# Searching the maxima of odd steps one step ahead, writing small maps in halves, moving keys and first values: one change to a two-layer convolution and attention kernel

## The chip, the cores and the metric

The kernel runs on one core of one Trainium2 chip. Its time is the device time of one execution in microseconds; the median of three runs is shown. The core has five engines with a queue of instructions each: TensorE (PE in the profile, with PEld for weight loads), VectorE (DVE), ScalarE (ACT), GpSimd (POOL) and SyncE (SP), which here only issues transfers. They meet through semaphores: an instruction waits until what it reads is there and what it overwrites has been read.

## The reference, cut to what matters

The input x has 8 images of 256 channels and 64 x 64 pixels, in float32. Two layers follow each other; each normalises its input by groups of 8 channels and adds its result to it.

Layer 0 makes, for every pixel, its own 3 x 3 filter and applies it:

```python
x1, x2, x3 = _conv1x1(x, w1, b1), _conv1x1(x, w2, b2), _conv1x1(x, w3, b3)   # 32, 32, 256 maps
h = jnp.concatenate([x1, unfold3(reflect(x2))], axis=1)
h = relu(bn2(_conv1x1(relu(bn1(h)), cw1)))
w = _conv1x1(h, cw2, cb2).reshape(B, 32, 9, H, W)
out = jnp.einsum('bgskhw,bgkhw->bgshw', x3u, w)      # 9 taps, one filter for 8 channels
```

Layer 1 adds two branches. The first is attention of four heads in a window of 7 x 7 around each pixel, with a position term added to the keys; the second applies two 3 x 3 depthwise convolutions with a relu between them and weighs the result by a softmax over nine branches:

```python
att = softmax(jnp.einsum('bdn,bdkn->bnk', q, uk + upe[None]))
out_att = jnp.einsum('bnk,bdkn->bdn', att, uv)
wts = softmax(jnp.einsum('oc,bchw->bohw', Wfc, x).reshape(b, C, 9, h, w), axis=2)
out_conv = sum over 9 of dwconv(relu(dwconv(x, w1)), w2) * wts
x + rate1 * out_att + rate2 * out_conv
```

## The kernel before, in words

An image is cut into 8 bands of 8 rows; 64 bands in all. Layer 1 works on band g while layer 0 prepares the band 12 ahead of it (`AHEAD`). The first 12 rounds therefore have layer 0 alone, the last 12 have layer 1 alone.

A round of one band has 8 steps: two halves of the channels (ct) times four (m). A step takes two tiles of 8 x 8 queries of two heads. The order of the work is written out by hand, in the loop at the end: every engine gets its instructions in the order in which the program records them, and `after(n, f)` puts f off by n places, of which each step has six (the calls of `advance`). `beside(g, s)` lists what a step carries besides its own work: `head` runs before the exponentials, `mid` in the middle, `end` at the end.

In a step PE makes: at even m the scores of this step and the next, both in one PSUM tile "sco" (L747); two products with the branch weights, "pf" (L883); the transposes of the step before, "ptp" (L784); at even m the weighted values of the two steps before, in a PSUM tile "small" (L796). DVE searches the maximum of each row of masked scores ("prob", "nmax", L761: two searches in a step, one for each head), ACT turns scores into exponentials (L769) and divides them by their sum (L778, after DVE's reciprocal "tot", L776), and turns pf into exponentials "ex" (L888). DVE also does the taps of the two depthwise convolutions ("acc", L840 and L866), and adds the attention to the band's result ("xr", L815).

Beside it stand:

- Layer 0's small maps (`small_maps` and `write_maps`): at step 0 PE makes 32 + 32 maps in the free half of "small" (L332), and ACT writes them to "x2" in eight pieces, four for each half of the band's rows (L347 and L351). POOL then copies border rows and columns (L355 to L364). `hidden_maps` reads x2 one round later (L422).
- Layer 0's 256 maps "p" (L373), half at the end of step 0 and half at step 1; ACT writes them to "x3n" (L378), from where they go to DRAM.
- The taps: at the end of steps 1 to 5 PE makes the filters of two taps, "pw" (L468); DVE multiplies the first at the next place and the second one place later ("prod", L481), POOL adds the products to "xg" (L489).
- Layer 1's keys (`keys`, PE "pk" L703, DVE "kb" L711 and L718), queries ("pq", "qb"), the position term "pe" (`position`, L655 to L661, made for the first image and stored for the others) and values (`values`, PE "pv" L598, ACT "vc" L605), which SP stores to DRAM ("vd", L618 and L622) and loads again as tiles "vt" (L640).

Four PSUM buffers with the tag "gen" go round among pf, ptp, p, pw, pk, pq and pv; "sco" and "small" have one buffer each. In SBUF, "vc" has one buffer and "ex" three.

The changed lines lie in `small_maps` and `write_maps`, `values`, `position`, `beside`, and the loop itself. What sets their order is, for the loop:

```python
prob, nmax = masked(nm, m, sco)         # each step searches its own maxima
for a, po in weighted:
    add_values(*a, po)
ahead = [f() for f in head]
tot = exponentials(nm, prob, nmax)
```

Of the kernel before, what the change touches and what calls it, by code (L numbers as in the profile page):

```python
# [18 lines left out]
P = 128  # L19
# [4 lines left out]
R = 8  # L24
# [63 lines left out]
def conv_layers_kernel(ctx: ExitStack, tc: tile.TileContext, ins: dict, out: bass.AP):  # L88
# [235 lines left out]
    def small_maps(b, i, home):  # L324


        im = images[b]

        p12 = home[:, 2 * P :].rearrange("p (r c) -> p r c", r=R // 2)
        for kt in range(NCT):  # L330
            for u in range(2):
                nc.tensor.matmul(  # L332
                    p12[64 * u : 64 * u + 64], im.w12s[:, kt, :],
                    im.xc[i][:, kt, u * BAND // 2 : (u + 1) * BAND // 2],
                    start=(kt == 0), stop=(kt == NCT - 1),
                )
        return lambda: write_maps(b, i, p12)

    def write_maps(b, i, p12):
        im = images[b]  # L340
        t = im.x2[i] = w0.tile([P, HR, W], F32, tag="x2", name=f"x2_{b}_{i}", bufs=2)
        bias = im.bias
        for u in range(2):
            r, o = u * R // 2, 64 * u
            for q, (dst, src) in enumerate(((1, 0), (0, 0), (0, 1))):
                n = W - (q != 1)
                nc.scalar.activation(  # L347
                    t[32 * q : 32 * q + 32, r + 1 : r + 1 + R // 2, dst : dst + n],
                    p12[o : o + 32, :, src : src + n], AF.Identity, bias=bias[o : o + 32, 0:1],
                )  # L350
            nc.scalar.activation(  # L351
                t[96:128, r : r + R // 2, :], p12[o + 32 : o + 64], AF.Identity, bias=bias[o + 32 : o + 64, 0:1]
            )

        nc.gpsimd.tensor_copy(t[0:32, 1 : 1 + R, 0:1], t[0:32, 1 : 1 + R, 2:3])  # L355
        nc.gpsimd.tensor_copy(t[64:96, 1 : 1 + R, W - 1 : W], t[64:96, 1 : 1 + R, W - 3 : W - 2])

        if i == 0:
            nc.gpsimd.tensor_copy(t[0:96, 0, :], t[0:96, 2, :])
        else:  # L360
            nc.gpsimd.tensor_copy(t[0:96, 0, :], im.x2[i - 1][0:96, R, :])
            nc.gpsimd.tensor_copy(im.x2[i - 1][0:96, R + 1, :], t[0:96, 1, :])
        if i == NB - 1:
            nc.gpsimd.tensor_copy(t[0:96, R + 1, :], t[0:96, R - 1, :])  # L364
# [218 lines left out]
    def values(b, j, half):  # L583

        im = images[b]
        if half == 0:
            im.vc[j] = w1.tile([P, R // 2, C], F32, tag="vc", name=f"vc_{b}_{j}", bufs=1)
        vc, yp = im.vc[j], im.yp[min(j, NB - 1)]  # L590
        first, last, _ = value_rows(j)
        pv = ps.tile([P, 2, C], F32, tag="gen", name=f"pv_{b}_{j}_{half}", bufs=4)
        for g in range(2):
            r = first + 4 * half + 2 * g
            if r >= last:
                break
            for kt in range(NCT):
                nc.tensor.matmul(  # L598
                    pv[:, g], yp[:, kt, r : r + 2].rearrange("p r c -> p (r c)"), wv[:, kt],
                    start=(kt == 0), stop=(kt == NCT - 1),  # L600
                )
            n = g + 1

        def take():
            nc.scalar.copy(vc[:, 2 * half : 2 * half + n], pv[:, :n])  # L605

        return take
# [39 lines left out]
    def position(b, i):  # L647

        first, last = new_keys(i)
        n, a = last - first, i * R + first  # L650
        pe = images[b].pe[i] = w1.tile([P, KW - PAD, W], F32, tag="pe", name=f"pe_{b}_{i}", bufs=1)
        if b:
            nc.sync.dma_start(out=pe[:, :n], in_=kept[i])
            return
        nc.gpsimd.tensor_add(  # L655
            pe[:, :n],
            pecol.unsqueeze(1).to_broadcast([P, n, W]),
            perow[:, a : a + n].unsqueeze(2).to_broadcast([P, n, W]),
        )
        kept[i] = dram.tile([P, n, W], F32, tag=f"pe{i}", name=f"pe_{i}", bufs=1)  # L660
        nc.sync.dma_start(out=kept[i], in_=pe[:, :n])  # L661

    kept = {}

# [259 lines left out]
    def beside(g, s):  # L924

        b, i = divmod(g, NB)
        bn, inx = divmod(g + 1, NB)
        head, mid, end = [], [], []

        early = i in (0, NB - 1)  # L930
        if g >= 0:
            if s == 2:
                mid.append(lambda: keys(b, i, 1) if early else queries(b, i, 1))
            if s == 3 and early:
                head.append(lambda: queries(b, i, 1))
            if s == 3 and not early:
                mid.append(lambda: keys(b, i, 1))
        edge = inx in (0, NB - 1)
        if 0 <= g + 1 < B * NB:
            if s == 5 - edge:  # L940
                mid.append(lambda: position(bn, inx))
            if s == 6:
                mid.append(lambda: keys(bn, inx, 0) if edge else queries(bn, inx, 0))
            if s == 7:
                head.append(lambda: queries(bn, inx, 0) if edge else keys(bn, inx, 0))

        made = [(b, i + 2, (4, 5))] if g >= 0 and i < NB - 1 else []
        if i == NB - 1 and 0 <= b + 1 < B:
            made = [(b + 1, 0, (3, 4)), (b + 1, 1, (5, 7))]
        for bb, j, d in made:  # L950
            if s in d and (j < NB or s == d[0]):
                mid.append(lambda bb=bb, j=j, d=d: values(bb, j, d.index(s)))
            if s == d[1]:
                end.append(lambda bb=bb, j=j: store_values(bb, j))
            if s == d[1] + 1 and j in (0, NB):
                end.append(lambda bb=bb, j=j: mirror_rows(bb, j))
            if s == 7 and j != 1:
                for u in range(NT // 2):
                    end.append(lambda bb=bb, j=j, u=u: value_tile(bb, j, u))
        if g >= 0 and i == 0 and s in (0, 2):  # L960
            for u in (s, s + 1):
                mid.append(lambda u=u: value_tile(b, 1, u))

        nxt = [(b, i + 2, 0)] if g >= 0 and i + 2 < NB else []
        if i == NB - 1 and 0 <= b + 1 < B:
            nxt = [(b + 1, 0, 0), (b + 1, 1, 2)]
        for bb, ii, d in nxt:
            if s == d:
                end.append(lambda bb=bb, ii=ii: load_rows(bb, ii))
            if s in (d + 1, d + 2):  # L970
                end.append(lambda bb=bb, ii=ii, d=d: normalise(bb, ii, s - d - 1))

        alone = g < 0
        if 0 <= g + AHEAD < B * NB:
            bq_, iq = divmod(g + AHEAD, NB)
            if alone and s == 0:
                mid.append(lambda: small_maps(bq_, iq, small_tile(f"{bq_}_{iq}"))())
            if s == (2 if alone else 0):
                (mid if alone else end).append(lambda: value_maps(bq_, iq, 0, alone))
            if s == (3 if alone else 1):  # L980
                mid.append(lambda: value_maps(bq_, iq, 1, alone))
        if 0 <= g + AHEAD - 1 < B * NB and s == (2 if alone else 1):
            bh, ih = divmod(g + AHEAD - 1, NB)

            def hidden():
                parts = hidden_maps(bh, ih, alone)
                if not alone:
                    convs.extend(parts)

            end.append(hidden)  # L990
        if 0 <= g + AHEAD - 2 < B * NB and s in TAPS_AT[g < -1]:
            u = TAPS_AT[g < -1].index(s)
            end.append(
                lambda: tap_weights(*divmod(g + AHEAD - 2, NB), u, g < -1, PRODUCTS_AT[g < -1][u])
            )
        return head, mid, end
# [24 lines left out]
    with tc.manual_schedule():  # L1021
# [17 lines left out]
        for n, f in enumerate(layer1_loads()):  # L1039
            after(4 * STEPS * (3 + n), f)  # L1040

        pending, before, conv, convs = [], None, None, []
        for g in range(-AHEAD, B * NB):
            b, i = divmod(g, NB)
            for s in range(STEPS):
                ct, m = divmod(s, NT // 2)
                head, mid, end = beside(g, s)
                steer(g, s)
                if g >= 0:
                    nm = f"{b}_{i}_{ct}_{m}"  # L1050
                    weighted = []
                    if m % 2 == 0:
# [3 lines left out]
                        small = small_tile(nm)  # L1056
                        weighted, pending = weigh_steps(pending, small), []
                        if s == 0 and g + AHEAD < B * NB:
                            mid.append(small_maps(*divmod(g + AHEAD, NB), small))
                        if s in (4, 6) and convs:  # L1060
                            convs.pop()(small)
                        if before is not None:
                            pending.append((before[:-1], transposed(nm, before[-1])))
                    prob, nmax = masked(nm, m, sco)
                    for a, po in weighted:
                        add_values(*a, po)
                ahead = [f() for f in head]
# [41 lines left out]
                advance()  # L1109
                for f in end:  # L1110
                    f()
                advance()
        for last in (before, None):
            for a, po in weigh_steps(pending, small_tile(f"end{last is None}")):
# [88 lines left out]
```

## Time and profile before

| what | value |
|---|---|
| median of three runs | 3902.41 us (3900.53 to 3902.47) |
| profiled execution, its own time | 3901.4 us |
| its span, first to last instruction | 3899.5 us |
| granted TensorE clock, mean | 0.994 |
| PE busy | 3774.0 us, 97% |
| DVE, POOL, ACT busy | 3415.8, 3118.1, 2809.8 us |
| first scores of layer 1 (L747, band 0) | 233.46 us |
| an ordinary band, with layer 0 beside it | 57.6 us |

The profile is one execution. A row of a view gives an engine, a line, an operation, and the tile that is written and those that are read; "idle before" is how long the engine stood still in front of it, and the name after the arrow is what ended the wait. Ends of matmuls are modelled, so that distances between their starts say more than their durations. All times are microseconds unless marked ns.

### The profile page before, as it was taken

To read this page: it belongs to the slowest core of one execution; us is meant where nothing else is said; L and a number is where in the kernel's file an instruction comes from. 1 tells how busy PE (TensorE), PEld (TensorE's weight loads), DVE (VectorE), ACT (ScalarE), POOL (GpSimd) and SP (SyncE) were. 2 spreads that over 40 slices of the span, in tenths; PEclk is the share of its full clock that TensorE was granted. 3 is DMA by queue.
4 is the path that set the end of the run, shared out by engine and by line. 5 is a ranking of instruction groups with operands and counts; after the bars stand their busy time and mean duration, and the time that the engine had idled before them with its cause. 6 is when DMAs were issued, how large, how long until landed. Compare 5 with 4: busy or idle time off the path is not lost.

```text
span 3899.5 us, 71759 instructions
## 1 busy us (share of the span) xinstructions
PE 3774.0 (97%) x24620; PEld 2112.0 (54%) x24620; DVE 3415.8 (88%) x7125; ACT 2809.8 (72%) x6770; POOL 3118.1 (80%) x2100
## 2 busy tenths in 40 slices
PE   6889999999999999999999999999999999999998
PEld 3445555555555555555555555555555555555554
DVE  6879999889988989899998998989988889978777
ACT  4457777777777777777777777777777777677776
POOL 4768888888987988888888888978988888955665
PEclk9999999999999999999999999999999999999999
DMA  8754544544544543544544544454543543332221
GB/s 247 211 162 128 142 113 126 155 124 113 136 127 131 148 120 104 151 137 118 145 112 136 143 124 116 132 145 119 139 113 102 145 123 101 89 94 81 78 66 37
DMA packets 438926, 490.14 MB, mean 126 GB/s; under 512 B 62016, under 2 KB 324256, under 8 KB 438304
## 3 DMA queue, kind: packets, MB, share of 16 engines
q1 hardware_dynamic: 421984, 469.79, 43.4%
q10 hardware_dynamic: 16576, 15.76, 1.3%
q8 instruction: 194, 3.18, 0.3%
q14 instruction: 172, 1.41, 0.1%
HBM read 343.76 MB, written 145.10 MB: 125 GB/s over the span
## 4 chain that ended last, share of the span: by engine, by line
PE 38%; POOL 22%; DVE 20%; ACT 10%; issue 5%; DMA 4%; SPq 0%; ACTq 0%; POOLq 0%; DVEq 0%
PE pf L883 18%; POOL xg L489 10%; POOL ex L1099 7%; DVE prod L481 6%; DVE rec L904 4%; DVE acc L866 4%; PE small L796 3%; ACT x L347 3%; PE pv L598 3%; PE ptp L784 3%; PE sco L747 3%; PE pq L681 2%; PE pk L703 2%; DMA x<-x3n 2%; ACT ex L888 2%
## 5 line engine op out<-in xcount | busy, mean ns | idle before, releaser
L883 PE MATMUL pf<-yp,c_wfc 128*128 128x512 f32 x4096 | 1916.3, 594 | 16.7 <-ACT ex L888 10.3
L489 POOL TENSOR_TENSOR xg<-xg,prod 128x1024 f32<-128x1024 f32 x549 | 1201.0, 2188 | 108.7 <-DVE prod L481 82.7
L883 PEld LDWEIGHTS pf<-yp,c_wfc 128*128 128x128 f32 x4096 | 738.6, 190 | 715.7 <-issue 628.4
L1099 POOL TENSOR_TENSOR ex<-ex,ex 128x1024 f32<-128x1024 f32 x384 | 908.2, 2365 | 68.7 <-ACT ex L888 65.2
L840 DVE SCALAR_TENSOR_TENSOR acc<-yp,c_chan,acc 128x504 f32<-128x504 f32 (+3 forms) x1104 | 775.8, 703 | 63.3 <-ACT acc L831 42.9
L481 DVE SCALAR_TENSOR_TENSOR prod<-pw,c_par,x3q 128x1040 f32<-128x1040 f32 x576 | 737.3, 1287 | 92.3 <-PE pw L468 47.8
L866 DVE SCALAR_TENSOR_TENSOR acc<-hid,c_chan,acc 128x504 f32<-128x504 f32 (+3 forms) x1024 | 751.5, 734 | 18.1
L888 ACT ACTIVATE ex<-pf 128x512 f32<-128x512 f32 x1024 | 602.3, 588 | 220.7 <-PE pf L883 204.4
L769 ACT ACTIVATE prob<-prob,nmax 128x196 f32<-128x196 f32 x1024 | 459.2, 451 | 205.2 <-DVE nmax L761 204.9
L778 ACT ACTIVATE prob<-prob,tot 128x196 f32<-128x196 f32 x1024 | 413.0, 452 | 262.0 <-DVE tot L776 259.9
L905 POOL TENSOR_TENSOR tot<-tot,rec 128x256 f32<-128x256 f32 x254 | 185.7, 731 | 413.4 <-DVE rec L904 407.3
L904 DVE RECIPROCAL rec<-tot 128x256 f32<-128x256 f32 x256 | 445.8, 1741 | 8.2 <-POOL tot L899 6.6
L786 ACT COPY pt<-ptp 112x512 f32<-112x512 f32 x511 | 295.0, 577 | 111.3 <-PE ptp L784 110.8
L761 DVE CUSTOM_DVE_ANT_0 prob<-sco,c_mask 128x196 f32<-128x196 f32 x1024 | 324.8, 355 | 27.1 <-PE sco L747 27.0
L784 PEld LDWEIGHTS ptp<-ident,prob 128*112 128x112 f32 x2044 | 227.3, 133 | 184.8 <-issue 154.7
L784 PE MATMUL ptp<-ident,prob 128*112 128x128 f32 x2044 | 319.5, 279 | 0.2 <-ACT vc L605 0.2
L796 PEld LDWEIGHTS small<-pt,vt 112*64 112x64 f32 x8144 | 258.5, 138 | 83.5 <-issue 75.4
L796 PE MATMUL small<-pt,vt 112*64 112x64 f32 x8144 | 294.1, 225 | 7.2 <-DMA vt<-vd 7.2
L373 PE MATMUL p<-xc,w3s 128*128 128x512 f32 x512 | 248.1, 608 | 12.6 <-ACT ex L888 12.6
L598 PE MATMUL pv<-c_wv,yp 128*128 128x256 f32 x1056 | 252.3, 381 | 1.7 <-ACT yp L570 1.7
L899 POOL TENSOR_SCALAR tot<-tot 128x512 f32<-128x512 f32 x127 | 243.6, 1918 | 11.1
L468 PEld LDWEIGHTS pw<-h2n,c_c 128*128 128x128 f32 x1152 | 176.1, 192 | 138.2 <-issue 122.3
(136 smaller groups left out, 4655.4 us busy)
## 6 DMA issues: line engine op xcount, KB each, us to landing
vt<-vd SPq DMA_DIRECT2D x512, 112.0 KB
x3q<-x SPq DMA_DIRECT2D x128, 264.0 KB
xc<-in_x SPq DMA_DIRECT2D x64, 512.0 KB
xg<-in_xg SPq DMA_DIRECT2D x64, 512.0 KB
yp<-x SPq DMA_DIRECT2D x128, 256.0 KB
xr<-x SPq DMA_DIRECT2D x64, 512.0 KB
out_x<-xr SPq DMA_DIRECT2D x64, 512.0 KB
xs<-in_x SPq DMA_DIRECT2D x57, 512.0 KB
```

The costliest lines, as they stand in the source:

```text
L481: nc.vector.scalar_tensor_tensor(prod[:, :, :RUN], pw[:, j, :RUN].unsqueeze(1).to_broadcast([P, SHARE, RUN]), par[:, PCB2 + k : PCB2 + k + 1],
L489: nc.gpsimd.tensor_add(im.xg[i], im.xg[i], rows(prod))
L769: nc.scalar.activation(prob[:, h, :NKEY], prob[:, h, :NKEY], AF.Exp, bias=nmax[:, h : h + 1], scale=-1.0, accum_out=tot[:, h : h + 1],)
L778: nc.scalar.activation(prob[:, h, :NKEY], prob[:, h, :NKEY], AF.Copy, scale=tot[:, h : h + 1])
L784: nc.tensor.transpose(ptp[:, h, ch], prob[:, h, ch * CHUNK : (ch + 1) * CHUNK], ident)
L796: nc.tensor.matmul(po[half[h], :, t * TQ : (t + 1) * TQ], im.vt[i + ch, m][:n, t, (2 * ct + h) * HD : (2 * ct + h + 1) * HD], pt[:n, h, ch ...
L840: nc.vector.scalar_tensor_tensor(o, yp[:, ct, ra + dr : rb + dr, ca + dc : cb + dc], chan[:, ct, CW1 + k : CW1 + k + 1], o, ALU.mult, ALU.add,
L866: nc.vector.scalar_tensor_tensor(o, hid[:, ra + dr : rb + dr, ca + dc : cb + dc], chan[:, ct, CW2 + k : CW2 + k + 1], o, ALU.mult, ALU.add,)
L883: nc.tensor.matmul(pf, wfc[:, kt, 2 * m + j, ct * P : (ct + 1) * P], images[b].yp[i][:, kt, PAD : PAD + R], start=(kt == 0), stop=(kt == N ...
L888: nc.scalar.activation(ex[:, j].rearrange("p (r c) -> p r c", r=R), pf, AF.Exp)
L904: nc.vector.reciprocal(rec, v)
L1099: after(4, lambda ex=ex, exb=exb: nc.gpsimd.tensor_add(ex, ex, exb))
```

## The change

Five things move; no computation is added or removed. Every engine issues the same instructions as before, and POOL in the same order.

1. Maxima. At the end of each even step, after its `end` work is recorded, the maxima of the odd step that follows are searched; the odd step uses them. On DVE this changes places only at steps 3 and 5, where the two searches now stand in front of the first tap's product (L481).
2. Small maps. `small_maps` returns a function of the half. In rounds with layer 1 the first half of the maps is written at step 0, the second at step 1, ahead of that step's other `mid` work; POOL's copies follow the second half.
3. Keys. In bands that are neither first nor last of an image, the keys of the second half of the channels move at step 3 from `mid` to `head`: pk stands on PE ahead of pf and ptp, and DVE's kb ahead of two taps and the reciprocal.
4. First values. In the round before band 0, the values of band 1 take their second half at step 6 instead of 7, ahead of the queries, and their stores follow at the end of step 6; their tile vc takes a buffer of "ex".
5. Position. The store of pe is put off by nine places, so that on SP it comes after the stores of vd, in band 0 after the loads of x3q.

```diff
+        im.x2[i] = w0.tile([P, HR, W], F32, tag="x2", name=f"x2_{b}_{i}", bufs=2)
-        return lambda: write_maps(b, i, p12)
+        return lambda u: write_maps(b, i, p12, u)
...
-    def write_maps(b, i, p12):
+    def write_maps(b, i, p12, half):
...
-        for u in range(2):
+        for u in half:
...
+        if half[-1] == 0:
+            return
...
-            im.vc[j] = w1.tile([P, R // 2, C], F32, tag="vc", name=f"vc_{b}_{j}", bufs=1)
+            tag, bufs = ("ex", 3) if (b, j) == (0, 1) else ("vc", 1)
+            im.vc[j] = w1.tile([P, R // 2, C], F32, tag=tag, name=f"vc_{b}_{j}", bufs=bufs)
...
-        nc.sync.dma_start(out=kept[i], in_=pe[:, :n])
+        after(9, lambda: nc.sync.dma_start(out=kept[i], in_=pe[:, :n]))
...
             if s == 3 and not early:
-                mid.append(lambda: keys(b, i, 1))
+                head.append(lambda: keys(b, i, 1))
...
-            made = [(b + 1, 0, (3, 4)), (b + 1, 1, (5, 7))]
+            made = [(b + 1, 0, (3, 4)), (b + 1, 1, (5, 7 if g >= 0 else 6))]
...
-                mid.append(lambda: small_maps(bq_, iq, small_tile(f"{bq_}_{iq}"))())
+                mid.append(lambda: small_maps(bq_, iq, small_tile(f"{bq_}_{iq}"))((0, 1)))
...
+                if s == 1:
+                    mid, maps = maps + mid, []
...
-                            mid.append(small_maps(*divmod(g + AHEAD, NB), small))
+                            write = small_maps(*divmod(g + AHEAD, NB), small)
+                            mid.append(lambda write=write: write((0,)))
+                            maps.append(lambda write=write: write((1,)))
...
-                    prob, nmax = masked(nm, m, sco)
+                    prob, nmax = masked(nm, m, sco) if m % 2 == 0 else odd
...
+                if g >= 0 and m % 2 == 0:
+                    odd = masked(f"{b}_{i}_{ct}_{m + 1}", m + 1, sco)
```

More of the change, by code (lines that the diff above doesn't have):

```diff
@@ L336, in small_maps @@
                 )
-        return lambda: write_maps(b, i, p12)
-    def write_maps(b, i, p12):
+        im.x2[i] = w0.tile([P, HR, W], F32, tag="x2", name=f"x2_{b}_{i}", bufs=2)
+        return lambda u: write_maps(b, i, p12, u)
+    def write_maps(b, i, p12, half):
         im = images[b]
-        t = im.x2[i] = w0.tile([P, HR, W], F32, tag="x2", name=f"x2_{b}_{i}", bufs=2)
-        bias = im.bias
-        for u in range(2):
+        t, bias = im.x2[i], im.bias
+        for u in half:
             r, o = u * R // 2, 64 * u
@@ L1040, in conv_layers_kernel @@
             after(4 * STEPS * (3 + n), f)
-        pending, before, conv, convs = [], None, None, []
+        pending, before, conv, convs, maps = [], None, None, [], []
         for g in range(-AHEAD, B * NB):
```

## The prediction

> **What bounds the kernel now.** I read four views in turn. First the page: its opening line and the row of busy time.
>
> ```profile
> span 3899.5 us, 71759 instructions
> PE 3774.0 (97%) x24620; PEld 2112.0 (54%) x24620; DVE 3415.8 (88%) x7125; ACT 2809.8 (72%) x6770; POOL 3118.1 (80%) x2100
> ```
>
> TensorE is the bound: 97% busy, and the slices say 9 tenths from the fourth on. So an edit is worth only what it takes out of the remaining waits of PE. Second, who PE waited for; the columns are microseconds in total, times, longest.
>
> ```profile
> PE p L373 <- ACT ex L888: 12.6, 52, 0.9
> PE small L796 <- DMA vt<-vd: 7.2, 2, 6.7
> PE pf L883 <- DVE prod L481: 6.4, 6, 1.1
> PE sco L747 <- DVE kb L718: 5.2, 29, 0.2
> ```
>
> The first line occurs 52 times: once in each of the first 52 bands, just those that still prepare layer 0. Third, one ordinary band (829.0 to 886.6) in order of time, PE and then ACT (start, duration, engine, line).
>
> ```profile
> 837.46 1.88 PE L883 MATMUL pf<-yp,c_wfc 128*128 128x512 f32 x4
> 839.18 0.60 PE L784 MATMUL ptp<-ident,prob 128*112 128x128 f32 x4
> 839.96 1.98 PE L373 MATMUL p<-xc,w3s 128*128 128x512 f32 x4 [0.18 <-ACT ex L888]
> 841.78 1.88 PE L883 MATMUL pf<-yp,c_wfc 128*128 128x512 f32 x4
> ```
>
> ```profile
> 835.48 1.40 ACT L347 ACTIVATE x<-small,bias 32x252 f32<-32x252 f32 x3
> 836.89 0.46 ACT L351 ACTIVATE x<-small,bias 32x256 f32<-32x256 f32 x1
> 837.36 1.43 ACT L347 ACTIVATE x<-small,bias 32x252 f32<-32x252 f32 x3
> 838.82 0.47 ACT L351 ACTIVATE x<-small,bias 32x256 f32<-32x256 f32 x1
> 839.31 0.60 ACT L888 ACTIVATE ex<-pf 128x512 f32<-128x512 f32 x1
> ```
>
> The page's idle column understates a wait, since ends on PE are modelled; I take distances between starts. ptp to p is 0.78 us here; ptp to a product that waits for nothing is 0.43 (853.78 to 854.21, same band). p to pf is 1.82; four matmuls elsewhere take 1.72 (837.46 to 839.18). So this place costs 0.35 + 0.10 = 0.45 us. Its cause stands in the ACT rows: eight small-map writes run from 835.48 to 839.29 ahead of the exponential that frees the PSUM buffer which p needs. Fourth, the queue of transfers in the first band.
>
> ```profile
> 224.64 0.32 SPq L661 DMA_DIRECT2D pe<-pe  x1
> 225.06 1.32 SPq L618 DMA_DIRECT2D vd<-vc  x2
> 240.86 5.62 SPq L640 DMA_DIRECT2D vt<-vd  x8
> 246.59 1.33 SPq L618 DMA_DIRECT2D vd<-vc  x2
> 247.97 4.07 SPq L622 DMA_DIRECT2D vd<-vc  x6
> 252.75 3.12 SPq L640 DMA_DIRECT2D vt<-vd  x4
> ```
>
> SP issues without a gap from 225 to 256; PE wants the last four tiles at 248.8 and gets the first at 255.78, the second at 256.95.
>
> [...] I therefore price starts, not busy time. [...] the exponential whose input is long ready starts 0.02 us after the eighth write. [...] here a value tile takes 3.0 us from issue to use (252.75 to 255.78).
>
> **Maps in halves.** Moved: four of eight writes per band, 4 x 0.47 = 1.9 us of ACT, from step 0 to step 1 behind the normalised probabilities. Added: nothing. The exponential then starts at 837.4 and ends at 838.0; p is wanted at 839.61. The wait goes. Summed over starts, ptp to p and p to pf exceed 0.43 and 1.72 by 0.45 us in 43 ordinary bands (19), and by 0.7 to 1.1 in eight at image edges or beside them (6): 25 us. Band 0 is counted below. Queued behind the moved writes are x3n, an exponential and the next hid. ACT from 839.31 to 843.05 runs 3.74 us without a gap; starting 1.9 earlier it runs the same 3.74 (nmax was ready at 837.5, tot waits for ACT alone, the product pf ends by 839.3), then the four writes, so x3n starts where it did, near 843.0. Waiting for the second half are two things: "small", single-buffered, which PE writes again at 844.89 - 0.45 = 844.4, a slack of 1.4 us; and POOL's four copies of border rows, now about 843.1 to 844.2 instead of 837.9 to 839.6. POOL idles 5.29 us there until 844.87, so the copies cost nothing; hid, which reads their rows, starts at 846.5. Without these covers the price is the lateness itself, per band.
>
> **Maxima earlier.** Two searches (2 x 0.28 us plus a 0.08 us readout, 0.65 in all) pass one tap product (1.21 us) at steps 3 and 5. The same DVE work; ACT's exponentials of these steps can start 1.2 us sooner, the product and POOL's addition 0.65 later. No PE wait above names nmax. PE's wait for the next scores' buffer gains room. I take 0; bounds -3 us (the product's buffers come free late: the third line of PE's waits) to +5 (a DVE that had idled for pw fills the gap, so the second product of step 5 ends sooner).
>
> **Keys at the head of step 3.** pk passes pf and ptp (1.72 + 0.43 us earlier on PE), and its four DVE operations, 0.65 + 3 x 0.15 = 1.1 us, now stand ahead of two depthwise taps and the reciprocal. In ordinary bands sco waits for kb: pw to sco is 0.79 (857.65 to 858.44) against 0.55 (843.49 to 844.04) where it waits for nothing, 27 times 0.24 = 6.5 us. After the change DVE does two searches, two products and the keys from 852.6: 0.65 + 2.4 + 1.1 is 856.8, before sco at about 858. The 6.5 goes. The price: the reciprocal, ACT's second exponential of step 3 and oc come up to 1.6 us later; PE next needs that buffer 3 us later. Unseen cost: 0 to 3 us; I take 0.
>
> **First values moved.** vc of band 1 gets a slot of "ex", so ACT need not wait 9.0 us (until 231.07) for the stores of vc of band 0; the second half of its product goes ahead of pq. The store of pe goes nine places later, so vd's stores need not wait for POOL's pe (224.64) but only for the copy of vc at 220.7. SP then issues: 8 stores of vd 4.6 us, xr 0.5, six x3q 3.9, pe 0.4, mirrors 1.9, the 8 stores of band 1 (5.5), xs 0.6, four x 3.3, eight tiles 5.6: the last four begin at about 247.0 instead of 252.75, and with the 3.0 to 3.2 us from issue to use PE has both by 250.9 instead of 256.95. PE itself starts band 0 two microseconds sooner (sco at 231.3 for 233.46, after qb, no longer behind vc), which the wait swallows. Gain 6; bounds 2 (only PE's earlier start, if SP stays clogged) to 8. In bands 1 to 7 pe's store, 0.4 us of SP, now follows eight stores of vd; pe is read from DRAM only an image later, so nothing waits.
>
> **Sum.** 25 + 6.5 + 6 = 37.5 us. At image edges DVE (first band) and POOL (last band) set PE's waits; both have their early idle shortened (DVE waits 2.55 us for tot at step 1, POOL 5.29), so the gain should pass through, though not all. I take off 1.5 for that: 36. The profiled execution took 3901.4, 1.9 over its span; the median of the runs is 3902.41, 1.0 above it. 3902.4 - 36 is 3866.
>
> **Rivals.** (A) The freed time comes back as waits for DVE or POOL, whose work per band is unchanged: in an ordinary band they are busy 52.4 and 49.6 of 57.6 us. For: the waits of pf for prod, and DVE runs without a gap through most of a first band. Against: both idle in steps 0 and 1. It would keep a third of the 25, and the rest: 3902 - 20 = 3882. (B) Slower: the second half of the maps is late, and PE waits for "small" at step 2 of every band. The slack is 1.4 us; each microsecond beyond costs 52. It decides from 0.9 us of stall (0.9 x 52 = 47 eats 38 + 8): the writes would have to end 2.3 us later than reckoned. At 1.5 us of stall: 3902 + 78 - 36 = 3944. Against: no gap in ACT's run between. (C) The transfers do not matter and the p wait only changes its releaser (x3n or pt instead of ex): within 8 us, 3900. For: four PSUM buffers stay four. Against: p takes the buffer of the fourth tile before it, which is pf's alone. (D) More: relief of DVE and POOL also removes the edge waits (PE for prod, by starts some 14 us): 3852. For: both engines then begin their dense stretch 0.6 to 1 us sooner. Against: PE does too, by 0.45.
>
> **Chances.** Forecast (3857 to 3876) 0.58, A 0.18, D 0.10, B 0.06, C 0.08. What runs of this kernel can tell is about 0.2%, 8 us. Faster: 0.58 + 0.18 + 0.10 + 0.01 of C = 0.87; same 0.07; slower 0.06. The range leaves out B, C and the tail of D: 3850 to 3888.
>
> **What would show it.** Right: p after ptp at 0.43 us and no line "p <- ex"; sco no longer waiting for kb; small's wait for vt down from 7.2 to about 3 us; ordinary bands of 56.9 us. Wrong: PE's "small" or pf waiting for ACT's L347 family at step 2; hid waiting for POOL's copies; pw waiting for kb at the end of step 3.

## The result and the profile after

The changed kernel takes 3855.64 us, the median of four runs (3854.63 to 3858.96), against 3901.80 for the kernel before beside it: a ratio of 0.9884, with a 95% interval of 0.9866 to 0.9901. Measured once more with the last experiments it took 3852.70 against 3901.10, a ratio of 0.9876 (0.9861 to 0.9890). The gain is 46 to 48 us; the forecast was 36. The profiled execution took 3854.63 us with a span of 3852.8.

First the page of the changed kernel: its opening line, the row of busy time and the head of the chain that ended last.

```profile
span 3852.8 us, 71646 instructions
PE 3756.3 (97%) x24620; PEld 2109.9 (55%) x24620; DVE 3434.4 (89%) x7125; ACT 2809.2 (73%) x6770; POOL 3116.8 (81%) x2100
PE 81%; POOL 10%; DVE 3%; DMA 2%; ACT 2%; issue 2%; SPq 1%; ACTq 0%; POOLq 0%; DVEq 0%
```

PE's share of the span is the same 97% as before: nothing of the gain can be seen in the share of busy time. The chain shows it. Before, PE carried 38% of the chain, POOL 22% and DVE 20%; now PE carries 81% of it. Half of the rest is POOL's.

Second, who PE waited for (total us, times, longest). These lines answer those shown of before; the longest waits of the list, left out here, lie in the rounds that have layer 0 alone.

```profile
PE pf L886 <- DVE prod L483: 6.3, 6, 1.1
PE pf L886 <- ACT ex L891: 4.4, 10, 1.1
PE pw L470 <- ACT ex L891: 1.8, 1, 1.8
PE small L799 <- DMA vt<-vd: 1.8, 1, 1.8
PE small L799 <- ACT x L351: 1.5, 1, 1.5
```

No line "p <- ex" is left, where there had been 52 waits, and no line "sco <- kb", where there had been 29. The waits of pf for prod are as they were. The wait for the value tiles fell from 7.2 us to 1.8, but two waits of the first band that did not exist before stand beside it. One of them, "small" waiting for ACT's map writes, is what the prediction named as a sign of being wrong; it occurs once in the kernel.

Third, one ordinary band (816.23 to 873.1) in order of time, PE and then ACT.

```profile
824.67 1.88 PE L886 MATMUL pf<-yp,c_wfc 128*128 128x512 f32 x4
826.38 0.60 PE L787 MATMUL ptp<-ident,prob 128*112 128x128 f32 x4
826.82 1.88 PE L375 MATMUL p<-xc,w3s 128*128 128x512 f32 x4
828.54 1.88 PE L886 MATMUL pf<-yp,c_wfc 128*128 128x512 f32 x4
831.65 1.15 PE L799 MATMUL small<-pt,vt 112*64 112x64 f32 x32
```

```profile
824.10 0.47 ACT L351 ACTIVATE x<-small,bias 32x256 f32<-32x256 f32 x1
824.58 0.60 ACT L891 ACTIVATE ex<-pf 128x512 f32<-128x512 f32 x1
828.45 1.43 ACT L347 ACTIVATE x<-small,bias 32x252 f32<-32x252 f32 x3
829.90 0.47 ACT L351 ACTIVATE x<-small,bias 32x256 f32<-32x256 f32 x1
```

From ptp to p is now 0.44 us (before 0.78), and from p to pf 1.72 (before 1.82). The exponential at 824.58 follows the fourth write instead of the eighth. The second four writes end at 830.37, and PE overwrites "small" at 831.65: the slack is 1.28 us, where 1.4 was reckoned.

A band's length, taken from its first scores to the next band's, tells more than a total of waits, since it needs no pace to compare with. The means over bands 1 to 51, by kind (i = 3 without band 51, which is as short as an ordinary one), in five profiles, three of them of kernels told of below:

| Bands | before | halves alone | keys alone | maxima alone | all |
|---|---|---|---|---|---|
| ordinary (i = 1, 2, 4, 5) | 57.6 | 56.9 | 57.6 | 57.6 | 56.9 |
| first of an image (i = 0) | 59.6 | 58.9 | 59.6 | 58.9 | 58.2 |
| i = 3 | 60.4 | 59.5 | 60.3 | 60.4 | 59.6 |
| i = 6 | 57.5 | 56.6 | 57.4 | 57.4 | 56.5 |
| last of an image (i = 7) | 61.3 | 60.8 | 61.4 | 61.4 | 60.8 |
| sum of bands 1 to 51 | 2987.2 | 2949.4 | 2987.3 | 2983.2 | 2945.0 |

The last twelve bands took 610.8 to 610.9 us in all of them: the change doesn't touch these.

### The profile page after: what moved, and what is told of

Same layout as the page of the kernel before. It is cut to its first block, busy times and chain, and to the rows that moved or that the text cites. A ratio compares the mean times of both kernels' runs of the same rounds, so it can differ in the third digit from the quotient of the medians.

```text
span 3852.8 us, 71646 instructions
## 1 busy us (share of the span) xinstructions
PE 3756.3 (97%) x24620; PEld 2109.9 (55%) x24620; DVE 3434.4 (89%) x7125; ACT 2809.2 (73%) x6770; POOL 3116.8 (81%) x2100
## 4 chain that ended last, share of the span: by engine, by line
PE 81%; POOL 10%; DVE 3%; DMA 2%; ACT 2%; issue 2%; SPq 1%; ACTq 0%; POOLq 0%; DVEq 0%
PE pf L886 39%; PE small L799 6%; PE ptp L787 6%; POOL xg L491 6%; PE pk L706 5%; PE pq L684 5%; PE sco L750 5%; PE p L375 5%; PE pv L601 5%; PE pw L470 2%; POOL ex L1106 2%; PE small L332 1%; DVE prod L483 1%; PE small L434 1%; DMA x<-x3n 1%
## 5 line engine op out<-in xcount | busy, mean ns | idle before, releaser
L483 DVE SCALAR_TENSOR_TENSOR prod<-pw,c_par,x3q 128x1040 f32<-128x1040 f32 x576 | 732.7, 1294 | 107.9 <-PE pw L470 60.8
```

The source lines that it names most:

```text
L483: nc.vector.scalar_tensor_tensor(prod[:, :, :RUN], pw[:, j, :RUN].unsqueeze(1).to_broadcast([P, SHARE, RUN]), par[:, PCB2 + k : PCB2 + k + 1],
```

## The experiments

### One part of the change at a time

Four kernels each hold one part of the change and are otherwise the kernel before. The first has the map writes in halves (of its edit, the lines in the loop):

```diff
+                if s == 1:
+                    mid, maps = maps + mid, []
...
-                            mid.append(small_maps(*divmod(g + AHEAD, NB), small))
+                            write = small_maps(*divmod(g + AHEAD, NB), small)
+                            mid.append(lambda write=write: write((0,)))
+                            maps.append(lambda write=write: write((1,)))
```

> The kernel before with the small maps' writes in halves alone. Theory (each part is worth the distances between PE's starts that it removes, and the parts don't interact): p follows ptp by 0.43 us in every band, the wait of p for ex goes, and 23 to 28 us go from the 3902. The waits of sco for kb (29) and of pf for prod in the bands at an image's edges stay as they were. Rival (freed time comes back as waits for DVE and POOL): pf, pw and small wait more, and no more than 18 us go.

Measured: 3864.67 us against 3901.51, a ratio of 0.9908 (0.9895 to 0.9922), so 30 to 41 us, 37 in the middle. That is more than the theory allowed, and the rival is off on the other side. The wait of p went as expected; by starts, ptp to p and p to pf had held 26.6 us and hold 0.2. The rest is in two places that this edit doesn't touch. The waits of sco for kb, which were to stay, went as well (6.6 us by starts): two are left, 0.5 us together. And the wait ahead of the statistics' products pg, in single bands of each image, shrank from 9.5 to 4.1 us by starts. The reason is in DVE's rows of step 1, first of the kernel before, then with the halves:

```profile
841.52 0.17 DVE L776 RECIPROCAL tot<-tot 128x2 f32<-128x2 f32 x1 [2.55 <-ACT prob L769]
```

```profile
832.36 0.17 DVE L778 RECIPROCAL tot<-tot 128x2 f32<-128x2 f32 x1 [0.63 <-ACT prob L771]
836.45 1.30 DVE L483 SCALAR_TENSOR_TENSOR prod<-pw,c_par,x3q 128x1040 f32<-128x1040 f32 x1 [0.84 <-PE pw L470]
```

Before, the eight writes also stood ahead of ACT's exponentials of the probabilities, and so DVE stood idle for 2.55 us until their sums came. From there it ran without a gap up to the keys' additions at step 3, which then came 0.24 us late for the next scores. With four writes moved, the sums come 1.9 us earlier (10.6 us after the band's start, for 12.5) and DVE even waits for pw again (0.84 us): it has caught up. The lateness of kb was the same ACT delay, handed on through 16 us of DVE work.

The second kernel moves the keys only:

```diff
             if s == 3 and not early:
-                mid.append(lambda: keys(b, i, 1))
+                head.append(lambda: keys(b, i, 1))
```

> The kernel before with the keys' matmuls of step 3 at the head of the step alone. Theory: the 29 waits of sco for kb go, pw to sco shortens by 0.24 to 0.28 us in each, 6 to 8.5 us go, and p still waits for ex 52 times. Rival (the DVE work of the keys only pushes the depthwise taps and the reciprocal back, and PE waits for these instead): between +1 and -3 us, with new waits of ptp or pw at step 4.

Measured: 3901.21 us, a ratio of 1.0001 (0.9993 to 1.0009). The waits of sco for kb all went, and nothing was gained: ordinary bands stay at 57.58 us. The rival is right that a wait takes their place, but it isn't at step 4's ptp or pw. Here are the lines of the same kernel around the second value product, at step 5 of the band that starts at 828.0:

```profile
869.22 0.60 ACT L888 ACTIVATE ex<-pf 128x512 f32<-128x512 f32 x1 [0.53 <-POOL ex L1099]
869.87 0.30 PEld L883 LDWEIGHTS pf<-yp,c_wfc 128*128 128x128 f32 x2 [0.40 <-ACT ex L888]
```

PE's weight load for pf waits for ACT's exponential, and that one for POOL's sum of exponentials. In the kernel before the same pf starts without a wait, because PE is still 0.24 us behind from the scores. POOL's sum (L1099) itself begins 38.8 us after the band's start in both kernels. So PE gains 0.24 us at the scores and, against a chain that hasn't moved, hands it back 11 us later: 0.26 us by starts, the mean of 26 ordinary bands (0.18 from pv to pf, 0.08 from pf to pw).

The third has the odd steps' maxima ahead of their step:

```diff
-                    prob, nmax = masked(nm, m, sco)
+                    prob, nmax = masked(nm, m, sco) if m % 2 == 0 else odd
...
+                if g >= 0 and m % 2 == 0:
+                    odd = masked(f"{b}_{i}_{ct}_{m + 1}", m + 1, sco)
```

> The kernel before with the odd steps' maxima ahead of the step alone. Theory as forecast: 0, between -2 and +2 us. Rival formed from the two traces (in the first band of each image PE's pf waits for DVE's product through pw's buffer, and a DVE that fills its idle time before pw with the maxima has its later product done sooner): 0.5 to 0.8 us less in each of the 8 first bands, mostly between pv and pf, 4 to 6 us in all, nothing in ordinary bands.

Measured: 3897.29 us, a ratio of 0.9990 (0.9982 to 0.9998), so 1 to 7 us. The size and the place are the rival's: the first bands are 0.7 us shorter and ordinary ones unchanged. The mechanism isn't. A first band of the kernel before shows at step 5:

```profile
754.15 0.46 ACT L769 ACTIVATE prob<-prob,nmax 128x196 f32<-128x196 f32 x1 [1.21 <-DVE nmax L761]
755.05 0.57 ACT L888 ACTIVATE ex<-pf 128x512 f32<-128x512 f32 x1
755.68 1.55 PE L883 MATMUL pf<-yp,c_wfc 128*128 128x512 f32 x3 [0.55 <-ACT ex L888]
```

and with the maxima moved, from the same place of its band:

```profile
751.52 0.46 ACT L769 ACTIVATE prob<-prob,nmax 128x196 f32<-128x196 f32 x1
752.88 0.60 ACT L888 ACTIVATE ex<-pf 128x512 f32<-128x512 f32 x1 [0.37 <-POOL ex L1099]
753.55 1.97 PE L883 MATMUL pf<-yp,c_wfc 128*128 128x512 f32 x4
```

PE waits for ACT's exponential of pf, that one queues behind the exponentials of the probabilities, and these wait for the maxima, which stand behind a tap's product on DVE. Moved ahead of that product, the maxima let ACT start these exponentials 1.2 us sooner in the band, and that of pf 0.7 us sooner; there it now waits for POOL's sum, which is the next limit. The list of PE's waits names only the last link: its line "pf <- ACT ex" falls from 10.3 us in 16 waits to 4.3 in 7. The price is in the same list:

```profile
PE sco L747 <- DVE kb L718: 12.9, 35, 1.2
PE sco L747 <- POOL xg L489: 4.0, 6, 0.7
```

The waits of sco grew from 5.2 to 16.9 us, while those ahead of pg (9.5 by starts) went.

The fourth has the moves of the first values and of the store of pe:

```diff
+            tag, bufs = ("ex", 3) if (b, j) == (0, 1) else ("vc", 1)
+            im.vc[j] = w1.tile([P, R // 2, C], F32, tag=tag, name=f"vc_{b}_{j}", bufs=bufs)
...
-        nc.sync.dma_start(out=kept[i], in_=pe[:, :n])
+        after(9, lambda: nc.sync.dma_start(out=kept[i], in_=pe[:, :n]))
...
-            made = [(b + 1, 0, (3, 4)), (b + 1, 1, (5, 7))]
+            made = [(b + 1, 0, (3, 4)), (b + 1, 1, (5, 7 if g >= 0 else 6))]
```

> The kernel before with the moves of the first values and of the store of pe alone. Theory: only band 0 changes, PE's wait of small for vt falls from 6.7 to about 2 us, and 4 to 6 us go. As in the changed kernel the load of xs stands behind vd's stores of the second block, DVE's statistics wait for it some 5 us in band 0, and PE waits for ACT (pw for ex, small for x) for about 3 us. Rival (the jitter of the transfers at the start is as large as the gain): 2 us or less.

Measured: 3894.45 us, a ratio of 0.9984 (0.9978 to 0.9991), so 4 to 9 us, 7 in the middle. The second band starts at 295.1 us, for 301.6 before; bands 1 to 51 last as long as before (2986.8). PE's wait for the tiles is 3.0 us, more than expected, and a wait of pw for ex of 0.8 stands beside it. The expected wait of "small" for x isn't there: it belongs to the halves, and stands with 1.5 us in the kernel that has these alone.

The four parts add up: 36.8 + 0.3 + 4.2 + 7.1 is 48.4 us, and the whole was 46.2 in its first measurement and 48.4 in its second.

### One part less

The changed kernel, with the keys put back to the middle of step 3:

```diff
             if s == 3 and not early:
-                head.append(lambda: keys(b, i, 1))
+                mid.append(lambda: keys(b, i, 1))
```

> The changed kernel with the keys of step 3 put back to the middle of the step. Theory N (in ordinary bands the wait of sco for kb was a lateness of DVE, which starts late because the statistics of ACT come late behind the map writes; the halves alone cure it): 0 to 3 us over the changed kernel, 3855 to 3859, ordinary bands stay at 56.9 us and no wait of sco for kb comes back. Forecast (the keys are worth their own 6.5 to 8 us): 3862 to 3864, and 27 waits of sco for kb of 0.2 us.

Measured: 3852.61 us against 3901.36, a ratio of 0.9879 (0.9864 to 0.9894). Ordinary bands stay at 56.85 us. Theory N said that no wait of sco for kb would come back. Eight do, 6.4 us together, but none in an ordinary band, and they take the place of others there (around pg, some 8 us by starts): bands 1 to 51 sum to 2944.1 us, for 2945.0 with the keys moved. The forecast's value for the keys is refuted; beside the halves, their move is worth nothing that can be measured.

And with the maxima put back:

```diff
-                    prob, nmax = masked(nm, m, sco) if m % 2 == 0 else odd
+                    prob, nmax = masked(nm, m, sco)
...
-                if g >= 0 and m % 2 == 0:
-                    odd = masked(f"{b}_{i}_{ct}_{m + 1}", m + 1, sco)
```

> The changed kernel with the odd steps' maxima put back into their own step. Theory N (the maxima fill idle time of DVE ahead of pw, and the product of tap 7 of a first band is done sooner): the wait of pf between pv and pf comes back in the 7 first bands, 0.7 to 0.8 us each, 3859 to 3862. Forecast (0): 3855.

Measured: 3859.30 us, a ratio of 0.9895 (0.9882 to 0.9909). First bands are back at 58.9 us, bands with i = 6 at 56.9, and bands 1 to 51 sum to 2950.5: 5.5 us for the maxima, where they gained 3.9 alone. (The expectation gives the reason that the third kernel had already put in doubt; the number follows from either.)

### How much a late half would cost

Two kernels test the rival in which the second half comes too late. The first writes all eight maps at step 1:

```diff
-                            mid.append(lambda write=write: write((0,)))
-                            maps.append(lambda write=write: write((1,)))
+                            maps.append(lambda write=write: write((0, 1)))
```

> The changed kernel with all eight map writes at step 1. The total of ACT's work up to the last write is the same, but ACT now waits for p (about 1.1 us) and for pf (0.2), work that the first four writes filled. Theory: the last write ends 1.3 us later, at 15.4 after the band's start, the slack of 1.27 us ahead of small at step 2 is used up, PE waits 0 to 0.3 us in each of 52 bands: 0 to 15 us over the changed kernel. Rival (slack is really larger, since PE waits only for a part of the writes): 0. Rival (a late map is paid in full): 1.3 x 52 = 68 us over.

Measured: 3906.74 us, a ratio of 1.0015 (1.0007 to 1.0023): 51 us over the changed kernel's first measurement, and slower than the kernel before. None of the three numbers holds. In an ordinary band ACT waits 0.4 us for pf and 1.1 for p, so the writes end at 15.88 after the band's start and "small" begins at 15.94 instead of 15.42: 0.5 us per band where 0 to 0.3 was expected. That is one half of the loss; the other is a second wait, which the kernel's list of PE's waits shows:

```profile
PE small L799 <- ACT x L351: 26.6, 52, 3.3
PE pf L886 <- DVE prod L483: 20.9, 33, 0.9
```

The addition of "small" on DVE and ACT's work behind the writes are late too, DVE's dense stretch shifts, and 38.7 us after the band's start pf waits for a tap's product. That is so in 27 bands; the other six waits of the line, in the last bands of images, were there before. Ordinary bands are 58.2 us, 1.36 longer: 0.52 for the stall and 0.84 for what follows from it.

The second leaves the first half where it is and moves the second half to the end of step 1:

```diff
-                    mid, maps = maps + mid, []
+                    end, maps = maps + end, []
```

> The changed kernel with the second four map writes at the end of step 1, behind x3n, the second exponential, hid and the depthwise start. Theory (the price that the forecast named for a late second half: lateness beyond the slack times 52): the writes end near 17.8 us after the band's start instead of 14.14, PE waits for small at step 2 some 2.4 us in 52 bands, 125 us over the changed kernel, near 3980. Rival (DVE and POOL set the band's length once PE is late, and PE's later waits shrink by as much): under 60 us over.

Measured: 4039.45 us, a ratio of 1.0358 (1.0344 to 1.0372), 184 us over the changed kernel. The writes end at 17.98 and PE waits 133.3 us for them in 52 bands, 2.54 in most: the slack and the price of the wait itself are right. Most of the other 51 us is no wait of any engine. One band of this kernel:

```profile
991.22 1.15 PE L799 MATMUL small<-pt,vt 112*64 112x64 f32 x32 [2.54 <-ACT x L351]
992.30 0.72 PE L787 MATMUL ptp<-ident,prob 128*112 128x128 f32 x4
992.81 3.55 PE L886 MATMUL pf<-yp,c_wfc 128*128 128x512 f32 x4
996.20 1.88 PE L684 MATMUL pq<-yp,c_wq 128*128 128x512 f32 x4
```

Four matmuls of pf take 3.39 us from start to start, where they take 1.72 elsewhere. The stretches of the same place (span, busy times of PE, PEld, DVE, ACT and POOL, granted clock, share of the DMA engines, GB/s) show what goes with it:

```profile
988.00:991.00 3.00, 0.67 (x16) 0.28 (x8) 1.72 (x5) 2.88 (x7) 0.38 (x2) 1.00 0.00 1
993.00:995.00 2.00, 2.00 (x4) 0.82 (x3) 1.97 (x4) 1.50 (x6) 1.74 (x2) 0.50 0.00 0
995.00:997.00 2.00, 2.00 (x4) 0.72 (x3) 2.00 (x3) 0.54 (x2) 2.00 (x2) 0.71 0.00 0
997.00:999.00 2.00, 2.00 (x6) 0.95 (x5) 1.97 (x6) 1.63 (x5) 2.00 (x2) 1.00 0.00 0
```

After the wait the granted clock is 0.50 from 993 to 995 and 0.71 from 995 to 997, and 1.00 again from 997. By distances between starts, 37 of the 52 bands lose 1.2 us or more behind the wait, mostly 1.5 to 1.7 (some 61 us in all, of which waits elsewhere give a little back); the other 15, with the same 2.5 us of idle time, lose nothing.

### The first band

The changed kernel was measured again beside the last runs, as it is:

> The changed kernel once more, beside the next two. 3854 to 3858; first scores of band 0 within 2 us of 233.6 (so much does the start move between runs whose start is the same code).

Measured: 3852.70 us (3850.15 to 3853.41), a little less than expected; the first scores came at 231.27, 2.4 us before those of the first profile. This kernel loads xs behind eight stores, as the first profile showed: DVE waits 5.7 us for the load with the maxima queued behind it. The next kernel puts xs ahead of the stores, and loads the value tiles in the order in which step 2 wants them:

```diff
-            if s == d[1]:
+            if s == d[1] and (g >= 0 or j != 1):
                 end.append(lambda bb=bb, j=j: store_values(bb, j))
+            if s == 7 and g < 0 and j == 1:
+                head.append(lambda bb=bb, j=j: store_values(bb, j))
...
-                for u in range(NT // 2):
+                for u in range(NT // 2 if g >= 0 else 2):
...
                 mid.append(lambda u=u: value_tile(b, 1, u))
+            if b == 0 and s == 0:
+                for u in (2, 3):
+                    mid.append(lambda u=u: value_tile(b, 0, u))
```

> The changed kernel with two transfers' places changed in band 0: the load of xs ahead of the stores of the second value block, and the value tiles in the order in which step 2 wants them (0 and 1 of both blocks before 2 and 3 of the first). Theory: DVE's statistics no longer wait 5.7 us for xs, PE's waits for ACT (pw for ex 1.8, small for x 1.5) and for vt (1.8) go or halve, band 0 shortens from 63.3 to 58 to 60 us, 3 to 5 us in all. Rival (one wait stands behind the other, the last tile or the products of POOL): under 1 us.

Measured: 3855.06 us, a ratio of 0.9886 (0.9869 to 0.9902): no gain, the rival. The waits for xs and for ACT's ex are gone and band 0 is no shorter, 64.7 us for 63.3 and 63.8. The wait that took their place, ACT first and then PE:

```profile
255.47 1.13 ACT L572 ACTIVATE yp<-yp,aff 128x896 f32<-128x896 f32 x1 [7.50 <-DMA yp<-x]
257.22 0.56 ACT L789 COPY pt<-ptp 112x512 f32<-112x512 f32 x1
```

```profile
PE pf L886 <- ACT pt L789: 3.9, 1, 3.9
```

PE needs the buffer that ACT's copy of ptp frees. That copy stands behind the normalised rows, whose loads stand behind twelve value tiles in SP's queue. The same kernel with the keys put back as in the experiment above:

> The same, and the keys of step 3 back in the middle of the step. If the keys' move is worth nothing beside the halves, the same as the run ahead within 3 us; if it is worth its 6.5 us, slower by that.

Measured: 3853.46 us (3850.34 to 3854.39), 1.6 under the run ahead: again nothing for the keys. The last kernel puts the six loads of the rows ahead of value tiles 2 and 3, which are wanted at step 4 only. Against the first of these two kernels:

```diff
-            if b == 0 and s == 0:
-                for u in (2, 3):
-                    mid.append(lambda u=u: value_tile(b, 0, u))
...
+        if g == 0 and s == 0:
+            for u in (2, 3):
+                end.append(lambda u=u: value_tile(0, 0, u))
```

> The run with the tiles' order, and the six loads of yp's rows put ahead of value tiles 2 and 3 of the first block. Theory (in band 0 PE's pf waits 3.95 us for ACT's pt, which stands behind the normalised rows yp, which wait for their loads behind twelve value tiles on SP): the rows come 2.8 us sooner, pf's wait falls from 3.95 to about 1 us, band 0 shortens from 64.7 to about 61.5 us. Rival (yet another wait stands behind it, small at step 4 for the value tiles or hid for the maps' store): band 0 stays within 1 us of 64.7.

Measured: 3849.91 us (3847.90 to 3851.72), a ratio of 0.9866 (0.9850 to 0.9883). Band 0 is 61.1 us, and PE's waits of this band are now, above all:

```profile
PE small L799 <- DMA vt<-vd: 2.7, 2, 1.9
PE pf L886 <- ACT pt L789: 0.7, 1, 0.7
```

The theory holds: 3.7 us of band 0. Its median is the lowest of all, 2.8 us under the changed kernel's second measurement; that difference is too small for the intervals to tell, and rests on the trace.

## Why the prediction was right in kind, and where it was wrong

**What bounds the kernel.** Right: only what left PE's waits counted, and distances between starts gave the price of a wait that the idle column showed as 0.18 us. Ordinary bands came out at 56.9 us, the forecast's number, but in part by luck: the 0.24 us at the scores came from the halves and not from the keys.

**Maps in halves, 25 us.** The wait itself was sized right (26.6 us by starts went). The term is 36.8 because of the last step, the sum: it treated the wait of sco for kb as a second, independent item, and took 1.5 off for edges on the ground that DVE and POOL set the end there. DVE was late at both because of the same eight writes. The view that says so was quoted for another purpose: DVE waits 2.55 us for the sums at step 1. Followed onward, it runs without a gap to the keys; followed backward, it waits for ACT. Rival D named this mechanism (both engines begin their dense stretch sooner), and was wrong on what it relieves: the waits of pf for prod in last bands stayed at 6.3 us.

**Keys, 6.5 us.** Wrong. The prices of the DVE work were right, and the wait of sco went, but the step "PE next needs that buffer 3 us later" looked for one buffer only. PE's gain met POOL's sum of exponentials 11 us later. In these kernels a band in which DVE and POOL run dense from step 1 to step 5 is as long as their chain, and a shift inside it moves the wait. What shortens it is an earlier start of the chain, and that the halves gave.

**Maxima, 0.** Wrong by 4 to 5.5 us, at the upper end of its bounds (+5). The step "no PE wait above names nmax" stopped one link too early: PE's wait named ex, and ex stood behind nmax on ACT.

**First values, 6 us.** Right: 7.1 alone. The times of the single transfers were met in the kernel with this part alone (PE has the tiles at 250.4, forecast 250.9) and missed in the first profile of the whole (253.7), whose start was 2.4 us later than that of the second profile of the same kernel, which has them at 251.0. What the step left out was the order behind the moved stores: it counted xs in SP's queue but not DVE behind xs. That cost nothing in the end: with xs and the tiles ahead, the tile-order run waits for the rows instead. The forecast also put at nothing what the halves do in band 0, where "small" waits 1.5 us for ACT's second half.

**Rival B.** The slack was right (1.28 for 1.4 us), the price was not: beyond the slack a late half costs 52 times the stall, and more in what follows. 0.5 us of stall made ordinary bands 1.4 us longer, through DVE; 2.5 us of stall, 133 us in all, cost 51 us on top, mostly in the 37 bands that lose behind the wait; in the one shown the granted clock is 0.50 there, and over the whole span it is 0.977, for 0.994 in the changed kernel.

The forecast was 10 to 12 us too cautious, from the halves (12 short), the maxima (4), the first values (1) and the edges (1.5 taken off), less the keys (some 6 too many). That the total came as near as it did is luck in part, since the 6.5 us put down to the keys were gained by the halves. The first measurement, 3855.6, lies just under the forecast's own 3857 to 3876, and both measurements lie nearer to rival D's 3852 than to 3866.

## What to carry to other kernels

When the bound engine waits, follow the releaser back along its own queue to where that engine last waited, and on from there, until work that nothing held up: waits in different places of a loop can be one delay handed on through a dense engine, and then the earliest cure takes all of them, while a cure at a later place only moves the wait. Before adding the gains of two edits, ask whether either would still be there if the other were made; a run of each alone, and of the whole without it, settles that. Price a new stall of TensorE above its own length: here 0.5 us of it made ordinary bands 1.4 us longer, as what queues behind it shifted too, and 133 us of stalls, with the granted clock at 0.50 behind the one shown, made the kernel 184 us longer.

## What was not expected of the hardware

The late-half run has a wait of some 2.5 us on PE in most of 52 bands. In the band shown above (991.22) the granted clock is 0.50 behind it, and four matmuls of pf take 3.39 us from start to start; 37 bands lose 1.2 us or more in this place, mostly 1.5 to 1.7. The mean granted clock of this run is 0.977, where that of the changed kernel is 0.994. In the other 15 bands the same wait is followed by no loss. One of these, PE's rows from the wait on and two stretches behind it, as above:

```profile
867.99 1.15 PE L799 MATMUL small<-pt,vt 112*64 112x64 f32 x32 [2.54 <-ACT x L351]
869.07 0.65 PE L787 MATMUL ptp<-ident,prob 128*112 128x128 f32 x4
869.55 1.88 PE L886 MATMUL pf<-yp,c_wfc 128*128 128x512 f32 x4
871.27 1.88 PE L684 MATMUL pq<-yp,c_wq 128*128 128x512 f32 x4
868.00:870.00 2.00, 2.00 (x38) 1.69 (x39) 0.81 (x3) 1.98 (x3) 2.00 (x4) 1.00 0.00 0
870.00:872.00 2.00, 2.00 (x6) 0.94 (x5) 1.97 (x3) 1.76 (x6) 1.92 (x2) 1.00 0.00 0
```

Here the granted clock is 1.00, and the same four matmuls take 1.72 us. No view shows what sets the two kinds of band apart. The kernel before had a granted clock of 0.50 too, in its first band, behind the wait for the value tiles:

```profile
250.00:255.70 5.70, 0.00 (x0) 0.00 (x0) 0.00 (x0) 0.00 (x0) 1.58 (x1) 0.80 0.19 51
255.70:258.00 2.30, 1.74 (x15) 1.44 (x16) 0.52 (x2) 0.00 (x0) 0.00 (x0) 0.50 0.60 178
258.00:260.00 2.00, 2.00 (x6) 0.97 (x5) 1.96 (x3) 0.00 (x0) 0.81 (x1) 0.50 0.85 272
```

The changed kernel's first profile still shows 0.50 there (253.7 to 256), the tile-order kernel 0.50 behind its wait for pt (257.8 to 260), and the last kernel 1.00 from 246 to 258. So a part of what a shorter wait is worth in band 0 goes with the clock, and the forecast did not count it. Of the last kernel's 3.7 us it is some 1.6 by an estimate: behind its wait for pt the tile-order kernel takes 3.33 us from start to start for four matmuls of pf (257.83 to 261.16), where they take 1.72 elsewhere.

The start moves from one execution to the next: in seven profiles of kernels that hold the moves of the first values and the same code up to there, the first scores came between 229.5 and 233.6 us; in four of kernels with the values in their old place, between 231.7 and 233.5. The earlier start of 2 us that the forecast named thus isn't shown, but the second band began between 292.0 and 297.0 in the seven, and between 300.1 and 301.8 in the four. The start moves in this way although bands 1 to 51 of the changed kernel agreed within 0.2 us in its two profiles (2945.0 and 2944.8). A gain of a few microseconds in band 0 must be read from the waits and from more than one profile.
